# A stack of four graph attention layers on one core: two graphs share every transfer and the order of work is planned anew

## The chip, the cores and the metric

The kernel runs on one core of a Trainium2 chip. The metric is the device time of one execution in microseconds, taken as the median over several runs. One further execution is recorded by the hardware profiler; its span and the durations of its instructions are what the text below reads. The engines are PE (matrix products, results in PSUM), PEld (loading of PE's stationary operand), DVE and ACT (elementwise work and row sums), POOL (elementwise work[...]) and SP, which here only issues transfers.

## The reference, cut to what matters

There are 128 graphs with 128 nodes and 512 features, each with its own 0/1 adjacency matrix. Four attention layers follow each other; each layer adds its result to its input and normalises the rows.

```
x = layernorm(x + gat0(x, adj))       # one head, no weights: attn @ x
x = layernorm(x + gat1(x, adj))       # (a) 4 heads: x @ W1 [512 x 1024], attn, + b1, elu
                                      # (b) 1 head: h @ W2 [1024 x 512], attn, + b2
x = layernorm(x + gat2(x, adj))       # 8 heads of 64: x @ W [512 x 512], attn
x = layernorm(x + gat3(x, adj))       # 1 head: attn @ x, elu
attn = softmax(where(adj, leaky_relu(s_src[i] + s_dst[j], 0.2), -inf))
```

The scores s_src and s_dst are products of the (projected) node features with vectors. Per graph there are 1 + 4 + 1 + 8 + 1 = 15 attention matrices of 128 x 128. All is float32.

## The kernel before

A graph is one tile of 128 rows. `graph(g)` (from L567) lists the operations of graph g: `first` (layer 0), the projection by `w1s`, `second` (four heads), `halves` (the product with W2), `third` (one head of layer 1, then layer 2 with eight heads and layer 3). Each entry is an `Op` with an engine, a duration that the planner uses, buffers read and written, and a function that emits the instructions.

**Attention.** `spread` (L589 to L598) turns columns of destination scores into rows: a DVE transpose, a transfer to DRAM (`row`), and a transfer that broadcasts the rows to all partitions (`db`). `attend` forms the matrix: ACT adds the source score and applies the leaky relu (L646), with the result z in SBUF; DVE subtracts z from the mask and takes the row minimum (L654, one instruction and one read of the accumulator per head); ACT takes the exponential with a row sum (L663). `turned` transposes 128 x 128 blocks: DVE transposes 32 x 32 squares (L607), one transfer writes them to DRAM (L612), and one reads them back in transposed block order (L617 or L622). PE then multiplies by the features (`mixed`, L725; `block`, L896; `heads`, L938).

**Projections.** `project` (L710) chains four matmuls of 128 rows per column group and evicts by ACT (L717). In `second` the four-head projection is 16 matmuls of 258 columns per graph: 512 columns for two heads plus four score columns, in two halves. The product with W2 covers two graphs together: `halves` computes a 2 x 2 block product by Strassen's scheme with seven products of four matmuls of 257 columns (L794) instead of eight. The sums of its left operands are POOL's (L780), the sums of W2's blocks are formed once in the setup. DVE adds partial results (L812), ACT copies others out of PSUM (L807). `norm` is DVE's statistics (L681, L682), ACT's inverse root (L685, L686), a small POOL instruction (L692, for layer 2 also L696) and ACT's scaling (L699). The scores of layer 3 are put together on DVE (L956 to L969).

**What sets the order.** `Pipeline.plan` places the operations of one graph in a period of 28 us, by urgency and with a random shift from a fixed seed. `Pipeline.run` repeats this for all graphs, each 28 us later, and `Pipeline.order` walks through all operations as a list scheduler: an engine takes the earliest operation that can start, not more than AHEAD = 20 us past the oldest one not yet issued. The engines then run their lists strictly in that order and wait on semaphores. Buffers of 128, 512 and 1024 elements a partition share three families of slots (`w128`, `w512`, `w1024`), others have their own; the eight PSUM banks are handed out one at a time. All transfers of the loop are issued by SP: 30 per graph.

**Setup.** Weights are loaded and completed with score columns in the same list, with written times of -20 to 205 us: W1 at once, W2's sums at 109, the eight-head weights `wha` between 70 and 205.

The functions that the change touches, with their lines:

Of the kernel before, what the change touches and what calls it, by code (L numbers as in the profile page):

```python
# [26 lines left out]

PERIOD = 28.0
LATENCY = {"PE": (0.0, 0.8), "DVE": (0.15, 1.44), "ACT": (0.1, 1.44), "POOL": (0.1, 1.44), "SP": (7.06, 7.06)}
FLOW = {"PE": (0.0, 0.6), "DVE": (0.15, 0.8), "ACT": (0.1, 0.8), "POOL": (0.1, 0.8), "SP": (4.5, 4.5)}
AHEAD = 20.0
URGENCY = 0.6
BANKS = 8

SEED, SPREAD = 989, 8.0


class Buf:


    def __init__(self, tag, shape, dtype=F32):
        self.tag, self.shape, self.dtype = tag, shape, dtype
        self.size = 1
        for d in shape[1:]:
            self.size *= d

        if dtype is F32 and shape[0] == P and self.size in (P, 4 * P, 8 * P) and not tag.startswith(("ps", "scr")):  # L50
            self.tag = f"w{self.size}"
        self.ap = self.slot = None

    def view(self, tl):
        if self.tag[0] == "w" and len(self.shape) > 2:
            dims = "abc"[: len(self.shape) - 1]
            tl = tl.rearrange(f"p ({' '.join(dims)}) -> p {' '.join(dims)}", **dict(zip(dims, self.shape[1:])))
        return tl


class Op:
    def __init__(self, engine, cost, emit, ins, outs, extra, uses=(), dma=0.0):
        self.dma = dma
        self.engine, self.cost, self.emit, self.extra = engine, cost, emit, extra
        self.wait = 0
        self.ins, self.outs = ins, outs
        self.uses = list(uses)
        self.bufs = list(dict.fromkeys([*ins, *outs, *uses]))

    def done(self, reader=None):  # L70
        own, other = LATENCY[self.engine]
        return self.cost + self.extra + (own if reader is self.engine else other)


class Pipeline:
    def __init__(self, make, n, place):
        self.make, self.n, self.place = make, n, place

    def plan(self, ops):


        before, after = [set() for _ in ops], [[] for _ in ops]
        last, readers = {}, {}
        for k, op in enumerate(ops):
            for b in op.ins:
                before[k].add(last[b])
            for b in op.outs:
                if b in last:
                    before[k].add(last[b])
                before[k].update(readers.get(b, ()))  # L90
            before[k].discard(k)
            for q in before[k]:
                after[q].append(k)
            for b in op.ins:
                readers.setdefault(b, set()).add(k)
            for b in op.outs:
                last[b], readers[b] = k, set()
        left = [0.0] * len(ops)
        for k in reversed(range(len(ops))):
            left[k] = ops[k].cost + max(  # L100
                (left[q] + ops[k].done(ops[q].engine) - ops[k].cost for q in after[k]), default=0.0
            )
        taken = {e: [] for e in LATENCY}
        times, ready, missing = [0.0] * len(ops), [0.0] * len(ops), [len(q) for q in before]
        waiting = [k for k in range(len(ops)) if not missing[k]]
        rng = random.Random(SEED)
        shift = [SPREAD * rng.random() for _ in ops]
        while waiting:
            k = min(waiting, key=lambda k: (ready[k] - URGENCY * left[k] + shift[k], k))
            waiting.remove(k)  # L110
            op, t = ops[k], ready[k]
            spans = taken[op.engine]
            while True:
                u = t % PERIOD
                clash = [
                    y + d - u for x, y in spans for d in (-PERIOD, 0.0, PERIOD)
                    if u < y + d - 1e-9 and x + d < u + op.cost - 1e-9
                ]
                if not clash:
                    break  # L120
                t += min(clash) + 1e-9
                assert t < ready[k] + 2 * PERIOD, "the period is too short"
            spans.append((t % PERIOD, t % PERIOD + op.cost))
            times[k] = t
            for q in after[k]:
                ready[q] = max(ready[q], t + op.done(ops[q].engine) + max(ops[q].wait, 0) * PERIOD)
                missing[q] -= 1
                if not missing[q]:
                    waiting.append(q)
        return times  # L130

    def run(self, setup):
        times, events = self.plan(self.make(None)), [(t, -1, k, op) for k, (t, op) in enumerate(setup)]
        for g in range(self.n):
            for k, op in enumerate(self.make(g)):
                if op is not None:
                    events.append((g * PERIOD + times[k], g, k, op))
        events.sort(key=lambda e: e[:3])
        for g, op in self.order(events):
            for b in op.outs:  # L140
                if b.ap is None and b.slot is not None:
                    b.ap = self.place(b, g)
            op.emit()

    def order(self, events):

        ops, n = [e[3] for e in events], len(events)
        ends, first, last, readers, open_uses = {}, {}, {}, {}, {}
        before, after = [0] * n, [[] for _ in ops]
        makes, coming = [[] for _ in ops], {}  # L150
        for i, op in enumerate(ops):
            need = {last[b] for b in op.ins + op.uses if b in last}
            for b in op.outs:
                need.update([last[b]] if b in last else [], readers.get(b, ()))
                if b not in first:
                    first[b] = events[i][0]
                    if b.tag != "const":
                        makes[i].append(b)
                        coming.setdefault(b.tag, []).append(i)
            need.discard(i)  # L160
            before[i] = len(need)
            for q in need:
                after[q].append(i)
            for b in op.ins + op.uses:
                readers.setdefault(b, []).append(i)
            for b in op.outs:
                last[b], readers[b] = i, []
            for b in op.bufs:
                open_uses[b] = open_uses.get(b, 0) + 1
                ends[b] = max(ends.get(b, 0.0), events[i][0] + op.done())  # L170

        free = {}
        for b, t in first.items():
            if b.tag != "const":
                places = free.setdefault(b.tag, [])
                s = next((s for s, e in enumerate(places) if e <= t), len(places))
                places[s : s + 1] = [ends[b]]
        assert len(free["ps"]) <= BANKS, "too few banks"
        free = {tag: [(0.0, s) for s in range(BANKS if tag == "ps" else len(p))] for tag, p in free.items()}
        ready, released, clock, lane = [0.0] * n, {}, {e: 0.0 for e in FLOW}, 0.0  # L180
        known = {e: [i for i in range(n) if not before[i] and ops[i].engine == e] for e in FLOW}
        issued, low, out = [False] * n, 0, []

        def start(i):
            t = max(clock[ops[i].engine], ready[i])
            for b in makes[i]:

                rank = 0
                for q in coming[b.tag]:
                    if q >= i or rank >= len(free[b.tag]):  # L190
                        break
                    rank += 1
                if rank >= len(free[b.tag]):
                    return None
                t = max(t, free[b.tag][rank][0])
            return t

        while len(out) < n:
            best = None
            for e, waiting in known.items():  # L200
                found = None
                for i in waiting:
                    if events[i][0] > events[low][0] + AHEAD and i != low:
                        break
                    t = start(i)
                    if t is not None and (found is None or t < found[0]):
                        found = (t, i)
                        if t <= clock[e]:
                            break
# [34 lines left out]
def tile_gat_stack(  # L244
# [63 lines left out]
    def mark():  # L308

        return Buf("const", [P, 1])  # L310
# [740 lines left out]
```

## Time and profile before

| | |
|---|---|
| median of 3 runs | 3246.22 us (3245.11 to 3246.83) |
| span of the profiled execution | 3258.4 us |
| PE busy | 3066.8 us (94%) in 14822 matmuls |
| DVE busy | 2779.0 us (85%) |
| ACT busy | 2451.2 us (75%) |
| POOL busy | 1895.1 us (58%) |
| transfers | 606.08 MB, 75.0% of the time of the 16 DMA engines |
| mean granted clock of PE | 0.976 |

A group of the profile is named by the line of kernel.py, the engine and the instruction, then output<-inputs by tile names, the shape, the count, the busy time, the mean length of one in ns, and the idle time of the engine before it with what ended it. Lengths of neighbours can overlap, so count x mean may exceed the busy time. Tiles of the three shared families all appear as `w`, PSUM banks as `ps`.

### The profile page before, as it was taken

What the parts mean: (1) busy time and instruction counts of PE and PEld (TensorE: products, weight loads), DVE (VectorE), ACT (ScalarE), POOL (GpSimd) and SP (SyncE); (2) the same over time, 40 slices, a digit from 0 to 9 for tenths busy, and PEclk for the clock granted to TensorE, in tenths of its full rate; (3) what the DMA queues carried; (4) which work ended last, traced back from release to release, by engine and by line L of the source; (5) the groups of instructions that cost most, each with busy time, mean ns of one, the idle gap of its engine ahead of it and who ended that gap; (6) DMA issues with size and microseconds to landing.
All of it is one profiled execution on the core that took longest, in us unless ns stands there. A gap on an engine that the chain in (4) does not pass through costs nothing. (4 is left out here: it accounts for less than half of the span.)

```text
span 3258.4 us, 62058 instructions
## 1 busy us (share of the span) xinstructions
PE 3066.8 (94%) x14822; PEld 2488.7 (76%) x14822; DVE 2779.0 (85%) x9833; ACT 2451.2 (75%) x8741; POOL 1895.1 (58%) x2347
## 2 busy tenths in 40 slices
PE   6899999999999999999999999999999999999984
PEld 4688887787777877877777778777787777878853
DVE  4779888888888988898888889889898898989875
ACT  2457787787777777787777877777877777778875
POOL 4655655665565655665555665565566556565533
PEclk7899999999999999999999999999999999999985
DMA  4358777877877877877778777877787787777875
GB/s 119 94 136 196 183 205 188 200 193 190 203 187 188 205 186 192 201 190 200 188 187 200 191 188 204 189 190 201 191 204 187 188 205 188 196 196 190 197 174 129
DMA packets 1657567, 606.08 MB, mean 186 GB/s; under 512 B 1311562, under 2 KB 1508170, under 8 KB 1657204
## 3 DMA queue, kind: packets, MB, share of 16 engines
q1 hardware_dynamic: 1655836, 598.97, 75.0%
q8 instruction: 120, 1.97, 0.2%
q14 instruction: 243, 1.99, 0.2%
q0 software_dynamic: 576, 2.10, 0.2%
q10 hardware_dynamic: 792, 1.06, 0.1%
HBM read 374.43 MB, written 227.48 MB: 185 GB/s over the span
## 5 line engine op out<-in xcount | busy, mean ns | idle before, releaser
L710 PE MATMUL ps<-w1s,w 128*128 128x258 f32 x4096 | 926.9, 384 | 48.5 <-DMA w<-scr 25.0
L710 PEld LDWEIGHTS ps<-w1s,w 128*128 128x128 f32 x4096 | 777.0, 191 | 186.3 <-DVE xl L812 39.5
L654 DVE CUSTOM_DVE_ANT_0 w<-w,w 128x128 f32<-128x128 f32 x1920 | 861.1, 544 | 65.6 <-ACT w L646 49.2
L794 PE MATMUL ps<-w2s,w 128*128 128x257 f32 x3584 | 849.0, 383 | 8.5 <-POOL w L780 8.4
L663 ACT ACTIVATE w<-w,nm 128x128 f32<-128x128 f32 x1920 | 748.0, 394 | 98.2 <-DVE nm L654 76.3
L794 PEld LDWEIGHTS ps<-w2s,w 128*128 128x128 f32 x3584 | 669.1, 191 | 188.8 <-issue 80.0
L646 ACT ACTIVATE w<-w,xl 128x128 f32<-128x128 f32 x1536 | 488.8, 389 | 279.9 <-DMA w<-row 259.1
L607 DVE STREAM_TRANSPOSE w<-w 128x512 f32<-128x512 f32 (+1 forms) x1024 | 551.5, 540 | 34.3 <-ACT w L663 13.3
L710 PE MATMUL ps<-wha,w 128*128 128x273 f32 x2048 | 502.3, 398 | 7.3 <-DMA w<-scr 6.9
L710 PEld LDWEIGHTS ps<-wha,w 128*128 128x128 f32 x2048 | 383.2, 192 | 87.4 <-DVE w L607 6.3
L699 ACT ACTIVATE w<-w,mr,rd 128x512 f32<-128x512 f32 x512 | 415.2, 811 | 33.9 <-POOL mr L692 33.0
L692 POOL TENSOR_SCALAR mr<-mv,rd 128x1 f32<-128x1 f32 x512 | 160.1, 313 | 409.4 <-ACT rd L686 201.8
L663 ACT ACTIVATION_READ_ACCUMULATOR w<-w,nm 128x1 f32 x1920 | 368.1, 192 | 0.0
L681 DVE BATCH_NORM_STATS2 st<-w 128x6 f32<-128x512 f32 x512 | 337.2, 668 | 5.4 <-POOL w L986 4.6
L881 POOL TENSOR_TENSOR xl<-xl,b1t 128x512 f32<-128x512 f32 x256 | 335.2, 1310 | 1.6
L938 PEld LDWEIGHTS ps<-xl,w 128*128 128x128 f32 x2048 | 274.3, 196 | 80.8 <-issue 24.4
L646 ACT ACTIVATE w<-w,sc 128x128 f32<-128x128 f32 x384 | 152.3, 397 | 227.6 <-DMA w<-row 226.6
L725 PE MATMUL ps<-w,w 128*128 128x512 f32 x512 | 277.4, 624 | 32.6 <-DMA w<-scr 31.6
L738 POOL TENSOR_SCALAR w<-adj 128x128 f32<-128x128 int32 x256 | 192.4, 752 | 188.2 <-DMA adj<-in_adj_dram 75.1
L717 ACT COPY xl<-ps 128x258 f32<-128x258 f32 (+1 forms) x768 | 273.2, 362 | 31.8 <-PE ps L710 31.3
L938 PE MATMUL ps<-xl,w 128*128 128x66 f32 x2048 | 265.2, 273 | 27.7 <-DMA w<-scr 14.4
L654 DVE DVE_READ_ACCUMULATOR2_ANT nm<- 128x1 f32 x1920 | 290.5, 151 | 0.0
(213 smaller groups left out, 4258.8 us busy)
## 6 DMA issues: line engine op xcount, KB each, us to landing
scr<-w SPq DMA_DIRECT2D x640, 256.0 KB
w<-scr SPq DMA_DIRECT2D x640, 256.0 KB
w<-row SPq DMA_DIRECT2D x128, 512.0 KB
w<-in_x_dram SPq DMA_DIRECT2D x128, 256.0 KB
w<-row SPq DMA_DIRECT2D x128, 256.0 KB
out_dram<-w SPq DMA_DIRECT2D x128, 256.0 KB
w<-row SPq DMA_DIRECT2D x384, 64.0 KB
scr<-w SPq DMA_DIRECT2D x384, 64.0 KB
```

Of the source, the lines that this page charges most:

```text
L607: op("DVE", 0.12 + 0.133 * n, lambda: nc.vector.transpose(zb.ap.rearrange("p b h c -> p h b c"), src.ap.rearrange("p (h b c) -> p h b c", ...
L646: nc.scalar.activation(z.ap[:, h, :], db.ap[:, h0 + h, :], AF.Prelu, bias=src(h0 + h), alpha=SLOPE)
L654: nc.vector.tensor_tensor_reduce(out=zz.ap[:, h, :].rearrange("p (b a) -> p a b", b=4), in0=z.ap[:, h, :].rearrange("p (a b) -> p a b", b= ...
L663: nc.scalar.activation(zz.ap[:, h, :], zz.ap[:, h, :], AF.Exp, bias=nm.ap[:, h : h + 1], scale=-1.0, accum_out=rs.ap[:, h : h + 1],)
L681: op("DVE", 0.6, lambda: nc.vector.bn_stats(st.ap, y.ap), [y], [st])
L699: op("ACT", 0.7, lambda: nc.scalar.activation(y.ap, y.ap, AF.Identity, bias=mr.ap, scale=rd.ap), [y, rd, mr], [y])
L710: op("PE", w * 4 / 2400 + 0.006, lambda k=k: nc.tensor.matmul(px.ap[:, :w], lhsT=lhs.ap[:, k, :], rhs=wa(k, c), start=(k == 0), stop=(k == ...
L717: op("ACT", 0.06 + w / 1200, lambda: nc.scalar.copy(dst(), px.ap[:, :w]), [px], [t])
L725: op("PE", width * 4 / 2400, lambda: nc.tensor.matmul(pa.ap[:, :width] if len(xv.shape) == 2 else pa.ap.rearrange("p (s c) -> p s c", s=2) ...
L794: return lambda: nc.tensor.matmul(q[b].ap[:, :C2], lhsT=x()[:, k, :], rhs=w2s[:, slot, k, :], start=(fresh and k == 0), stop=(k == 3), ski ...
L881: op("POOL", 1.3, lambda nh=nh: nc.gpsimd.tensor_add(xl.ap[:, nh, : 2 * FH], xl.ap[:, nh, : 2 * FH], b1t[:, nh * 2 * FH : (nh + 1) * 2 * F ...
L938: op("PE", 0.225, lambda u=u, h=h: nc.tensor.matmul(pa.ap[:, u * CH : (u + 1) * CH], lhsT=pt.ap[:, u, :], rhs=xl3.ap[:, h * CH : (h + 1) * ...
```

## The change

The list scheduler, the plan and most of the operations' list are written anew. What differs in the work:

- The unit is a pair of graphs. Every transfer carries both: x, adj, the result, each block transposition (`turned` takes several sources) and each spreading of scores. Layer 2's two groups of four heads of one graph share one transposition. Masks are made for two graphs in one POOL instruction, and the mask of layer 2 is made a second time in `fourth` from a fresh load of adj. The offsets and the score sums of layer 3 for both graphs are small POOL instructions; the latter were DVE's.
- `strassen` replaces both `halves` and the four-head `project`: the pair's two graphs are the rows of the 2 x 2 block product. For the four-head projection it runs twice (two column halves of 258), with two matmuls per product; `w1s` gets seven slots, and `combined` forms the block sums in the setup. The eight-head projection stays a plain product per graph.
- z, the leaky relu's result, is a PSUM bank instead of an SBUF buffer.
- A matmul chain is one operation of the planner instead of one per matmul.
- `plan` gives each operation a due time: the latest start along the longest path to the pair's end, stretched by 1.36, plus 45 us per pair. `lay_out` schedules by due times, with AHEAD = 30, and reckons with POOL and DVE keeping each other waiting (`port`), with descriptor times of transfers and with at most eight transfers under way. At most two Strassen products are open at once.
- Buffers of 64 elements a partition or more lie in one SBUF tile, the arena, at offsets found from the planned times; space is reused 2 us after its planned release.
- The setup's written times end at about 115 us instead of 205.

```diff
+STRETCH, PACE, AHEAD = 1.36, 45.0, 30.0
+HOP = {"PE": 0.0, "DVE": 0.0, "ACT": 1.0, "POOL": 1.0, "SP": 3.0}
+BANKS, PRODUCTS = 8, 2
+LANES = 8
+SLACK = 2.0
...
+def plan(ops):
...
+    for k in reversed(range(len(ops))):
+        left[k] = ops[k].least() + HOP[ops[k].engine] + max((left[q] for q in after[k]), default=0.0)
+    rng = random.Random(SEED)
+    return [STRETCH * (max(left) - left[k]) + SPREAD * rng.random() for k in range(len(ops))]
+
+def lay_out(ops):
...
+            free, best, limit = clock[e], None, ops[line_up[low]].due + AHEAD
+            if e == "SP" and len(landed) >= LANES:
+                free = max(free, landed[-LANES])
+            for due, i in line:
+                t = max(free, ready[i])
+                if due > limit:
+                    break
...
+                if best is None or t < best[0] - REACH:
+                    best = (t, i)
...
+    for b in sorted((b for b in used if b.arena), key=lambda b: (-b.size, b.began)):
...
+            if q.began < b.until + SLACK and b.began < q.until + SLACK:
+                if q.slot - b.slot >= b.size:
+                    break
+                b.slot = max(b.slot, q.slot + q.size)
...
-    w1s = const.tile([P, 4, 2, N1], F32, name="w1s")
+    w1s = const.tile([P, 7, 2, N1], F32, name="w1s")
...
+    w1_ready = combined(18, w1s, w1_ready, ["DVE", "DVE", "DVE", "DVE"])
...
+    def attend(db, h0, nh, src, mask, scaled=False):
+
+        z = bank()
...
+        op("ACT", [0.4] * nh, prelu, [db, src[0]], [z])
+        op("DVE", [0.24] * nh, masked, [z, mask[0]], [zz, nm])
+        op("ACT", [0.387] * nh, exp, [zz, nm], [zz, rs])
...
+    def strassen(left, s, w, nk, wide, cols, to, out, ready):
+
+        pa, pb, pc = bank(), bank(), bank()
...
+        product(pa, left[0][0], 0, True)
...
+        taken(pa, t1)
+        product(pc, left[0][1], 1, True)
+        added(pc, t1, 0, 0)
+        product(pa, s[1], 4, False)
+        product(pb, s[0], 3, True)
+        taken(pa, u2)
+        taken(pb, v)
+        product(pa, s[2], 5, False)
+        product(pb, s[3], 2, False)
+        added(pa, v, 1, 1)
+        added(pb, u2, 0, 1)
+        product(pa, left[1][1], 6, False)
+        copied(pa, wide, lambda: to(1, 0), joins=[out[1]])
...
+        def normed():
+            nc.gpsimd.tensor_add(sc4.ap, sc4.ap, sz.ap)
+            nc.gpsimd.tensor_mul(sc4.ap, sc4.ap, rd.ap.unsqueeze(2).to_broadcast([P, 2, 2]))
+            nc.gpsimd.tensor_mul(sw.ap, swf.ap.unsqueeze(1).to_broadcast([P, 2, 2]), md.ap.unsqueeze(2).to_broadcast([P, 2, 2]))
+            nc.gpsimd.tensor_add(sc4.ap, sc4.ap, sw.ap)
...
+    def pair(n):
+        st = first(n)
+        xT = st["xT"]
+        xl = [Buf("xl1", [P, 2, N1]) for _ in G]
+        left = [[part(xT, slice(4 * g + 2 * a, 4 * g + 2 * a + 2)) for a in range(2)] for g in G]
+        s = sums(left, [P, 2, P])
+        for j in range(2):
+            cols = slice(j * C1, (j + 1) * C1)
+            strassen(left, s, w1s, 2, C1, cols, lambda g, h, cols=cols: xl[g].ap[:, h, cols], xl, w1_ready)
+        hT = second(st, xl)
+        xl2 = Buf("xl2", [P, 2, 2, C2])
+        left = [[part(t) for t in both] for both in hT]
+        strassen(left, sums(left, [P, 4, P]), w2s, 4, C2, slice(0, C2), lambda g, h: xl2.ap[:, g, h, :], [xl2, xl2], w2_ready)
+        third(st, xl2)
...
```

## The prediction

> **What bounds the kernel now.** I read the engine totals first, then windows of the span, the rows of the steady stretch, the waits, and one stretch of the timeline. Windows over the ramp, the steady part and the drain (busy us and instruction count for PE, PEld, DVE, ACT, POOL, then clock and DMA share):
>
> ```profile
> 0.00:150.00 150.00, 111.17 (x382) 76.49 (x382) 89.18 (x259) 51.55 (x157) 92.04 (x98) 0.82 0.40 108
> 150.00:300.00 150.00, 147.80 (x728) 124.08 (x726) 120.40 (x387) 97.38 (x338) 80.44 (x89) 1.00 0.64 155
> 300.00:3000.00 2700.00, 2609.49 (x12856) 2135.26 (x12855) 2376.62 (x8493) 2115.03 (x7597) 1613.76 (x2008) 1.00 0.79 194
> 3000.00:3258.00 258.00, 198.32 (x862) 152.84 (x860) 192.79 (x697) 187.22 (x653) 108.82 (x154) 0.82 0.69 167
> ```
>
> In the middle 2700 us PE is busy 96.6% at full clock; DVE follows with 88%, DMA 79%, ACT 78%, POOL 60%. One graph issues 115 matmul instructions (each f32 matmul is two: 32 first projection, 28 second, 16 third, 6 mixing, 16 and 16 for the heads, 1 turn), so 12856/115 = 111.8 graphs passed: 24.15 us a graph, 48.3 a pair of graphs, 46.7 of it PE busy and 1.6 idle. The ramp and the drain cost the rest: 3258.4 - 64 x 48.3 = 167 us.
>
> Rows of PE and of the two dearest groups of DVE and ACT in the steady stretch (busy us, mean ns, idle before and its releasers):
>
> ```profile
> L710 PE MATMUL ps<-w1s,w 128*128 128x258 f32 x3583 | 805.8, 383 | 47.7 <-DMA w<-scr 25.0 <-DVE ri L671 9.3 <-DVE st L681 8.4
> L794 PE MATMUL ps<-w2s,w 128*128 128x257 f32 x3136 | 740.2, 382 | 1.4 <-POOL w L780 1.4
> L654 DVE CUSTOM_DVE_ANT_0 w<-w,w 128x128 f32<-128x128 f32 x1677 | 742.6, 539 | 47.2 <-ACT w L646 30.9 <-DMA row<-w 11.2 <-ACT w L663 3.8
> L646 ACT ACTIVATE w<-w,xl 128x128 f32<-128x128 f32 x1338 | 426.0, 389 | 262.5 <-DMA w<-row 241.8 <-issue 7.0 <-DVE mv L682 4.3
> ```
>
> A matmul instruction against w1s occupies PE for 805.8/3583 = 0.225 us; one against w2s, a column narrower, takes 0.236, so about 0.011 x 56 = 0.6 us a pair is waiting that the busy figure hides. PE's visible waits are small and spread: operands still in a transfer, or late from DVE. ACT waits mainly for broadcast rows in flight.
>
> The timeline shows why DVE is long (start, length; first DVE's masked sums, then POOL in the same stretch):
>
> ```profile
> 1601.14 1.26 DVE L654 CUSTOM_DVE_ANT_0 w<-w,w 128x128 f32<-128x128 f32 x1
> ...
> 1602.25 1.19 DVE L654 CUSTOM_DVE_ANT_0 w<-w,w 128x128 f32<-128x128 f32 x1
> ...
> 1603.30 1.42 DVE L654 CUSTOM_DVE_ANT_0 w<-w,w 128x128 f32<-128x128 f32 x1
> ...
> 1604.57 0.37 DVE L654 CUSTOM_DVE_ANT_0 w<-w,w 128x128 f32<-128x128 f32 x1
> ```
> ```profile
> 1600.88 1.27 POOL L862 TENSOR_TENSOR w<-w,b2t 128x512 f32<-128x512 f32 x1
> 1602.11 1.09 POOL L673 TENSOR_TENSOR w<-w,ri 128x512 f32<-128x512 f32 x1
> 1603.16 1.31 POOL L780 TENSOR_TENSOR w<-w,w 128x512 f32<-128x512 f32 x1
> ```
>
> Each long masked sum ends just after the POOL instruction that overlaps it; the one without such an overlap takes 0.37 us. The median of the line is 0.382, the mean 0.539.
>
> **What the Trainium skill says.** "SBUF — State Buffer", section "Who interferes with whom": a VectorE instruction with two SBUF inputs contends with a GpSimd instruction that reads SBUF and the later one blocks for the whole instruction; with at most one SBUF input, outside the two-port modes, it does not. The timeline agrees: 1.19 to 1.42 us against 0.37. "ScalarE: Activation LUTs", section "Step-by-step: what each stage is for": ScalarE writes PSUM with lower latency than SBUF. No ACT instruction of this trace writes PSUM. "PSUM — Partial Sum Buffer", section "PSUM bank collisions raise a hardware error": two engines may not touch one bank in the same partitions at once, whatever the columns. No run here shows that yet; it bears on a bank that ACT fills and DVE drains. "DMA: Bandwidth & Descriptors", section "Anatomy of one DMA — SWDGE (gpsimd) path": about 2 us of a transfer are fixed. It is said of GpSimd-issued transfers; the shortest on the chain of waits here, SP-issued, takes 2.57 us for 64 KB, which is close.
>
> **The change part by part**, per pair of graphs.
>
> *PE.* Strassen on the four-head projection: 2 column halves x 7 products x 2 = 28 f32 matmuls for 32, 8 instructions less: 8 x 0.225 = 1.8 us. Everything else keeps count and width (second 28, third 16 of 273 columns, mixing 6, heads 16 and 16). Two graphs in one transpose changes nothing. PE busy: 46.7 - 1.8 = 44.9. Sum of this part: 64 x 1.8 = 115 us.
>
> *DVE*, now 2376.6/2700 x 48.3 = 42.5. With its first input in PSUM a masked sum has one SBUF input: 30 x (0.539 - 0.382) = -4.8. The four tail score instructions go to POOL or merge: L959, L969 and L966 at 0.636, 0.270, 0.252, twice: -2.3. Fewer reciprocals (9 for 12 at 0.142), one mask product and one score shift for two: -0.8. Nine Strassen additions instead of four, at the 0.403 of L812: +2.0. Sum 36.6. Whether a PSUM input slows the sum is not shown; L903 with one takes 0.663 for 512 columns, L681 without takes 0.667, so I take nothing; bounds -1 and +2.
>
> *ACT*, now 37.8: 16 evictions for 15, +0.36. Prelu into PSUM is unknown: from -0.1 us each (the skill's hint, sized by guess from the 0.389 of L646) to +0.075 (four of them take 1.26 us in the timeline, 0.315 apiece, because they overlap; without overlap each is 0.389). So -3 to +2.2; I take +1.5. Sum 39.7.
>
> *POOL*, now 28.9: four operand sums of 256 columns at half of L780's 1.28, +2.6; masks of 256 columns, four for six of 0.75 to 0.83, +0.5; six small score instructions at about the 0.26 of L696, +1.6; norm offsets, eight small ones for ten, -0.9. Sum 32.7.
>
> *Transfers.* A graph now issues 30 on SP (the page's issue counts of the loop sum to 3840); a pair will issue 4 + 11 + 16 = 31 for 60. At medians of 0.42 to 0.64 us each that frees some 15 us of SP a pair, and 29 fixed latencies. Bytes stay, so DMA share rises with the pace only: 0.79 x 48.3/45.7 = 0.83. A transfer of eight heads lasts longer than one of four, but the order has about ten pairs in flight (the plan spreads a pair's steps over some 450 us of due time and starts one every 45), which covers it; without that cover each of the six doubled round trips costs 2 to 3 us on a pair's chain, which is paid only in the drain.
>
> *Order and arena.* They have no instructions. They decide how much of PE's waiting stays: 1.6 visible + 0.6 hidden a pair. DVE gets slack (88% to 80%), SP gets slack, ACT loses some (78% to 87%). I take half the 2.2 as recovered, less 0.3 for new waits (coarser hand-offs, arena space reused 2 us after its planned release): -0.8. Bounds: +2 and -2.2.
>
> *Ramp and drain.* Weights are due earlier (the last at 115 instead of 205), and the seven w1s slots need four more subtractions first, about 4 x 1.2 = 5 us, hidden behind the first graph's attention. Pairs enter two graphs at a time, and after the last third projection a longer eight-head chain runs alone, where PE cannot be filled: +15. The ramp should give about that back. I take 0, bounds -40 and +60.
>
> **Sum.** Pace 48.3 - 1.8 - 0.8 = 45.7; 64 x 45.7 = 2925; plus 167 = 3092 us of span, against 3258.4. The median of the runs stands at 3246.2/3258.4 = 0.9963 of the span: 3081, say **3080**.
>
> **Rivals.** (1) *PE stops waiting*: 44.9 less the hidden 0.6 is 44.3 a pair. 64 x 44.3 + 155 = 2990 of span, 2980; up to 3035 for the case. For it: ten pairs in flight, and an order that reckons with the shared port. Against: DVE at 80% and ACT near 87% in fixed order have never run without waits here.
> (2) *The gain goes into the ends and new waits*: the Strassen saving stands, nothing of the waiting is recovered, the ends cost +60: 64 x 46.5 + 227 = 3203, 3190; 3130 to 3235.
> (3) *Slower, by the bank hand-off*: ACT fills a bank with four heads, and DVE may not read the first head until the fourth is written, while the new order books them head by head. In order, DVE stands while it waits: at the 0.315 a head of today's prelu, 0.95 for each of six four-head attentions and 0.3 for each of three two-head ones, 6.6 us a pair, DVE 43.2 of 45.7, still no bound. It decides when DVE's standing passes 48.3 - 36.6 = 11.7 us a pair, that is 1.3 an attention, because ACT's prelus are queued behind other exponentials: 12.5 us give a pace of 49.1 and 3298. Against: DVE has other ready work most of the time.
> (4) *No change*: only by a chance cancellation of these.
>
> **How the numbers follow.** Forecast 0.52 (own range 3035 to 3130), rival 1 0.13, rival 2 0.17, rival 3 0.16, rival 4 0.02. Differences under 0.2% are about what a measurement of this kernel cannot tell from none. Faster 0.82, same 0.02, slower 0.16. The range 3000 to 3220 leaves out part of rival 1, the top of rival 2 and rival 3, about 0.2.
>
> **What would show it.** Right: 3584 matmul instructions in the first projection for 4096; masked sums with a mean near 0.4 us and a PSUM input; 1984 loop transfers on SP for 3840; a steady pace of 45 to 46.5 us a pair with PE at 97% or more; DVE near 80%. Wrong: masked sums waiting on the prelu for more than 10 us a pair; a ramp or drain over 200 us together; ACT over 95%; PE waits on transfers above 100 us in the steady part.

## The result, and the profile after

The changed kernel takes 3542.16 us (median; 3540.49 to 3544.96) against 3246.52 us: a ratio of 1.0903, 95% interval 1.0878 to 1.0928. It is slower by 296 us, and outside the forecast range. (A fourth run of the kernel before moved its median from the 3246.22 us above.)

The windows of the changed kernel over the ramp and the steady part, in the columns shown for before:

```profile
0.00:300.00 300.00, 229.56 (x943) 175.66 (x944) 186.01 (x588) 132.61 (x428) 161.44 (x175) 0.88 0.50 123
300.00:2800.00 2500.00, 2251.77 (x10600) 1811.23 (x10598) 1774.83 (x6670) 1801.48 (x6100) 1435.17 (x1903) 0.95 0.79 179
```

A pair now issues 222 matmul instructions, so 10600/222 = 47.75 pairs pass in 2500 us: 52.4 us a pair against 48.3 before and 45.7 forecast. PE is busy for 47.2 of them, at a granted clock of 0.95, and idle for 5.2. No other engine is full either: DVE 71%, ACT 72%, POOL 57%, DMA 79%.

The steady rows of PE, DVE and ACT (300 to 3200 us) that answer to those of before:

```profile
L710 PE MATMUL ps<-w2s,arena 128*128 128x257 f32 x3110 | 771.8, 402 | 198.7 <-DVE arena L755 178.8 <-DVE nm L653 12.6 <-ACT arena L718 4.8
L710 PE MATMUL ps<-w1s,arena 128*128 128x258 f32 x3080 | 762.7, 400 | 86.5 <-ACT ps L646 40.5 <-ACT arena L718 17.9 <-DVE arena L939 16.0
L653 DVE CUSTOM_DVE_ANT_0 arena<-ps,arena 128x128 f32<-128x128 f32 x1668 | 451.6, 380 | 84.8 <-ACT ps L646 50.9 <-issue 29.8
L646 ACT ACTIVATE ps<-arena 128x128 f32<-128x128 f32 x1328 | 487.4, 370 | 140.0 <-DMA arena<-row 79.3 <-DVE arena L939 20.9 <-DVE nm L653 7.3
```

The masked sum (now L653) fell from a mean of 0.539 to 0.380 us, as worked out, and the leaky relu into PSUM from 0.389 to 0.370. But the instructions against w1s and w2s are longer in the mean (0.400 and 0.402 us for 0.383 and 0.382), and PE waits for DVE's additions.

The lines that the rest of the text names: L597 is DVE's transpose of score columns (sT), L601 the transfer of the score rows to DRAM, L606 their broadcast; L619, L623 and L632 are the block transpose on DVE, its write to DRAM and its read-back; L672 is POOL's scaling by the inverse row sum, L755 the Strassen additions, L879 the elu, L939 the scaling of the eight heads, L718 ACT's evictions, L807 the load of x. Why DVE is late, the waits of POOL, DVE and SP say (what waited, for what, us in total, times, longest):

```profile
POOL arena L672 <- DMA row<-arena: 293.3, 48, 8.1
...
DVE arena L619 <- POOL arena L672: 235.5, 87, 8.7
DVE arena L619 <- DMA row<-arena: 120.4, 19, 7.8
DVE arena L939 <- DMA row<-arena: 99.2, 28, 10.4
...
SPq L601 <- DMA arena<-row: 263.7, 54, 6.9
...
SPq L601 <- DMA arena<-in_x_dram: 88.8, 36, 3.7
```

L601 sends the score rows to DRAM. It reads columns that DVE has just transposed (sT). It has no business with a load of x into another buffer, nor L672, a product of two buffers on chip, with a row transfer. Yet L601 waits for other transfers into the arena, 137 times in 55.4 pairs, and L672, L619 and L939 wait for L601's transfer. The timeline of SP shows one such place, and POOL, DVE and PE behind it (start, length, idle before):

```profile
1524.88 2.97 SPq L807 DMA_DIRECT2D arena<-in_x_dram  x1
1531.72 0.56 SPq L601 DMA_DIRECT2D row<-arena  x1
```
```profile
1533.65 1.61 POOL L672 TENSOR_TENSOR arena<-arena,ri 128x256 f32<-128x256 f32 x2 [6.94 <-DMA row<-arena]
```
```profile
1534.30 0.45 DVE L619 STREAM_TRANSPOSE arena<-arena 128x256 f32<-128x256 f32 x1 [7.43 <-POOL arena L672]
```
```profile
1536.37 3.79 PE L710 MATMUL ps<-w2s,arena 128*128 128x257 f32 x8 [5.80 <-DVE arena L755]
```

SP issues nothing between 1527.85 and 1531.72, where L601 waits 3.7 us for the load of x; then POOL, DVE and PE resume one after the other, after 6.9, 7.4 and 5.8 us.

### The profile page after: what moved, and what is told of

The parts are those of the page before. It is cut to its first block, busy times and chain, and to the rows that moved or that the text cites. A ratio compares the mean times of both kernels' runs of the same rounds, so it can differ in the third digit from the quotient of the medians.

```text
span 3541.5 us, 56054 instructions
## 1 busy us (share of the span) xinstructions
PE 3079.7 (87%) x14310; PEld 2463.1 (70%) x14310; DVE 2438.6 (69%) x9073; ACT 2440.3 (69%) x8229; POOL 1977.9 (56%) x2603
## 3 DMA queue, kind: packets, MB, share of 16 engines
q10 hardware_dynamic: 792, 1.06, 0.1%
## 5 line engine op out<-in xcount | busy, mean ns | idle before, releaser
L710 PE MATMUL ps<-w2s,arena 128*128 128x257 f32 x3584 | 888.4, 402 | 233.6 <-DVE arena L755 198.3
L710 PEld LDWEIGHTS ps<-w2s,arena 128*128 128x128 f32 x3584 | 702.0, 200 | 385.9 <-DVE arena L755 213.6
L710 PE MATMUL ps<-w1s,arena 128*128 128x258 f32 x3584 | 885.6, 400 | 94.3 <-ACT ps L646 42.9
L710 PEld LDWEIGHTS ps<-w1s,arena 128*128 128x128 f32 x3584 | 700.3, 199 | 302.3 <-issue 60.7
L718 ACT COPY arena<-ps 128x258 f32<-128x258 f32 (+2 forms) x1024 | 356.6, 374 | 726.6 <-PE ps L710 272.5
L619 DVE STREAM_TRANSPOSE arena<-arena 128x512 f32<-128x512 f32 (+1 forms) x832 | 504.5, 629 | 444.3 <-POOL arena L672 266.5
L662 ACT ACTIVATE arena<-arena,nm 128x128 f32<-128x128 f32 x1920 | 742.7, 394 | 6.3 <-DVE nm L653 6.2
L646 ACT ACTIVATE ps<-arena 128x128 f32<-128x128 f32 x1536 | 563.0, 370 | 165.0 <-DMA arena<-row 97.7
L653 DVE CUSTOM_DVE_ANT_0 arena<-ps,arena 128x128 f32<-128x128 f32 x1920 | 520.1, 380 | 130.6 <-ACT ps L646 87.0
L733 POOL TENSOR_TENSOR arena<-arena 128x256 f32<-128x256 f32 (+1 forms) x512 | 490.4, 975 | 151.9 <-issue 98.2
L710 PE MATMUL ps<-wha,arena 128*128 128x273 f32 x2048 | 499.8, 395 | 25.3 <-DMA arena<-scr 25.3
L672 POOL TENSOR_TENSOR arena<-arena,ri 128x512 f32<-128x512 f32 (+1 forms) x192 | 172.5, 913 | 394.6 <-DMA row<-arena 312.5
L653 DVE DVE_READ_ACCUMULATOR2_ANT nm<- 128x1 f32 x1920 | 289.1, 151 | 0.0
```

The lines of the kernel that those rows point to most:

```text
L619: op("DVE", 0.075 + 0.134 * m, lambda a=a, src=src: nc.vector.transpose(zb.ap[:, :, a * m : (a + 1) * m, :].rearrange("p b h c -> p h b c" ...
L646: nc.scalar.activation(z.ap[:, h * P : (h + 1) * P], db.ap[:, h0 + h, :], AF.Prelu, bias=src[1]()[:, h : h + 1], alpha=SLOPE)
L653: nc.vector.tensor_tensor_reduce(out=zz.ap[:, h, :].rearrange("p (b a) -> p a b", b=4), in0=z.ap[:, h * P : (h + 1) * P].rearrange("p (a b ...
L662: nc.scalar.activation(zz.ap[:, h, :], zz.ap[:, h, :], AF.Exp, bias=nm.ap[:, h : h + 1], scale=-1.0, accum_out=rs.ap[:, h : h + 1],)
L710: nc.tensor.matmul(px.ap[:, :w], lhsT=lhs(k), rhs=rhs(k), start=(fresh and k == 0), stop=(k == nk - 1), skip_group_check=True,)
L718: op("ACT", 0.04 + w / 1200, lambda: nc.scalar.copy(to(), px.ap[:, :w]), [px], outs, joins)
```

## The experiments

Theory A: the arena is one tile, and a read of sT out of it (every 32nd partition) is ordered by the program's semaphores against accesses to other parts of the tile, so that one score transfer waits for whatever is under way into the arena and later writers wait for it. Theory B: SP, in its fixed order, waits behind the larger transfers. Theory C: the hand-off of PSUM banks from ACT to DVE costs the time.

The experiments fall into three series on three chips, on which the kernel before took 3223, 3259 and 3252 us; with the result above it took 3247. So each ratio is to the kernel before of the same series, and times from different series can be compared to about 1% only.

**e1_scores_own**

```diff
-SLACK = 2.0
+SLACK = 1.5
...
-        self.arena = shape[0] == P and self.size >= 64 and tag not in ("ps", "const") and not tag.startswith("scr")
+        self.arena = shape[0] == P and self.size >= 64 and tag not in ("ps", "const") and not tag.startswith(("scr", "sT"))
```

> The changed kernel with the transposed score columns (sT) in tiles of their own instead of the arena; to make room, arena space is reused 1.5 us after its planned release instead of 2.0. Order and instructions are the same. Theory A (the read of sT out of the arena is taken to touch all of it, so that one score transfer per pair waits for all transfers under way into the arena and later writes wait for it): SP's waits of L601 on other loads and the waits of POOL and DVE on that transfer go, PE idles 1.5 to 2.5 us a pair instead of 5.2, the pace falls from 52.3 to 46.5 to 48 us, time 3160 to 3270. Theory B (SP's fixed order with transfers twice as large makes everything stand behind read-backs): the waits move to L632 and L606, time 3450 to 3540. Theory C (the PSUM bank hand-off of the leaky relu): no change, 3540.

Measured: 3096.15 us, ratio 0.9615 (0.9591 to 0.9638). It is faster than both kernels, and faster than theory A's own range. Its windows:

```profile
300.00:2800.00 2500.00, 2475.25 (x12320) 2037.21 (x12319) 2086.69 (x7769) 2094.47 (x7088) 1694.34 (x2221) 1.00 0.91 208
2800.00:3093.00 293.00, 204.69 (x952) 162.53 (x951) 172.72 (x654) 194.24 (x647) 133.23 (x195) 0.82 0.71 151
```

12320/222 = 55.5 pairs, 45.05 us a pair, PE busy 99% at full clock. SP's waits in its steady part (300 to 2800 us):

```profile
SPq L632 <- DMA scr<-arena: 206.4, 88, 4.7
SPq L601 <- DVE arena L755: 173.0, 47, 7.4
SPq L606 <- DMA row<-sT: 137.1, 70, 3.8
```

SP still waits for read-backs, as long as before (L632 had 246.6 us in 2900), and it costs nothing now: theory B falls. L601 no longer waits for other transfers. Theory C had required no change and falls too.

**e1b_scores16_own and e1c_slack**

```diff
-        self.arena = shape[0] == P and self.size >= 64 and tag not in ("ps", "const") and not tag.startswith("scr")
+        self.arena = shape[0] == P and self.size >= 64 and tag not in ("ps", "const") and not tag.startswith(("scr", "sT16"))
```

with SLACK at 1.9 (e1b); only SLACK at 1.5 (e1c).

> As e1_scores_own, but only the 16-row sT of the eight-head layer leaves the arena (space reused after 1.9 us). Theory A, if only that one transfer is at fault: within 1% of e1_scores_own. If the smaller ones matter too: between it and 3540. Theories B and C: 3450 to 3540.

> The changed kernel with space of the arena reused 1.5 us after its planned release instead of 2.0, nothing else. Theory A: the reuse distance is not the cause, 3540 within 1%. Rival D (reuse of arena space before its late readers are done is the cause): slower, 3580 or more.

Measured: e1b 3246.9 us, 1.0073 (1.0049 to 1.0097). In its trace L601 still waits 286 us of 2500 for broadcast rows on their way into the arena, so the smaller score transfers seem to matter too; the run also has another SLACK than e1_scores_own, and its time alone doesn't show it. e1c 3249.18 us, 1.0085 (1.0055 to 1.0116). This missed both expectations: reusing space earlier did no harm, but it took 293 us off. It moves buffers to other offsets and makes the arena narrower (32192 elements a partition for 32744), so it could not tell which of the two did it. With the same SLACK and on the same chip e1_scores_own is 153 us faster than e1c: that much goes with sT's own tiles, though these move the other buffers again. The next runs change the width alone.

**e5_arena_24_wider, e6_arena_1_wider, e9_arena_16_wider**

```diff
-        arena = work.tile([P, max(b.slot + b.size for o in order for b in o.bufs if b.arena)], F32, name="arena")
+        arena = work.tile([P, 24 + max(b.slot + b.size for o in order for b in o.bufs if b.arena)], F32, name="arena")
```

with 24, 1 and 16. Offsets, instructions and order stay; only the waits that the program gets differ.

> The changed kernel with the arena 24 elements wider (32768 for 32744 a partition), nothing else: every buffer lies at the same offset, every instruction and the order are the same. Counted in the compiled programs, the transfer of the 16 score rows waits on 0.05 other transfers on average instead of 4.95, the two-row ones on 0.40 instead of 1.25. Theory A in its sharper form (the width decides which strided reads out of the arena are taken to meet other parts of it): pace 45 to 46 us a pair, PE over 97% busy in the steady part, time within 1.5% of e1_scores_own, 3080 to 3150. Theory A' (what lies in the arena is reused too early, and moving sT out only shifted the places): no change, 3540.

> The changed kernel with the arena one element wider (32745), nothing else. In the compiled program the 16-row transfer waits on 4.98 others, the two-row ones on 3.36 instead of 1.25. Theory A: slower than the changed kernel, 3600 to 4000, since three more score transfers per pair wait for what is under way. Theory A': 3540.

> The changed kernel with the arena 16 elements wider (32760). In the compiled program the waits are as in the changed kernel (4.95, 1.25 and 1.06 other transfers for those of 16, 2 and 8 rows). If the waits decide and not the width as such: 3540 within 1%. If any widening helps: 3140.

Measured:

| arena, elements a partition | other transfers that a score transfer of 16, 2, 8 rows waits on (mean, in the compiled program) | us | ratio and interval |
|---|---|---|---|
| 32744 (the change) | 4.95, 1.25, 1.06 | 3542.16 | 1.0903 (1.0878 to 1.0928) |
| 32745 (e6) | 4.98, 3.36, 0.58 | 4319.2 | 1.325 (1.3223 to 1.3277) |
| 32760 (e9) | 4.95, 1.25, 1.06 | 3547.4 | 1.0901 (1.0861 to 1.0941) |
| 32768 (e5) | 0.05, 0.40, 0.98 | 3137.66 | 0.9627 (0.9611 to 0.9643) |

The unneeded waits decide. Twenty-four unused elements take 404 us off (415 by the ratios), one adds 777, and sixteen, which leave the waits as they were, change nothing. The traces show the difference as well. These are the separate wait instructions of L601 and its transfers in 2500 us, first of the changed kernel, then of e6 and of e5:

```profile
L601 SPq EVENT_SEMAPHORE  x325: 17/28/3674, 299.2 to 2797.0; - x163
L601 SPq DMA_DIRECT2D row<-arena x239: 521/556/2200, 300.6 to 2797.1; - x120
```
```profile
L601 SPq EVENT_SEMAPHORE  x486: 17/28/10828, 306.2 to 2794.4; - x162
L601 SPq DMA_DIRECT2D row<-arena x192: 503/554/573, 308.2 to 2794.4; - x192
```
```profile
L601 SPq DMA_DIRECT2D row<-arena x275: 533/555/2122, 306.1 to 2798.3; - x138
L601 SPq EVENT_SEMAPHORE  x113: 17/17/860, 308.6 to 2796.9; - x113
```

That is 1.4, 2.5 and 0.4 waits a transfer. Counted as in the table, e1c has 0.95, 0.32 and 0.95 and e1b 0.05, 1.41 and 1.05: e1c had lost most of the 16-row transfer's waits without meaning to, and e1b had kept those of the two-row ones. e6 went beyond its expected 4000. Its ACT waits in the steady part show the row transfers in front of everything:

```profile
ACT arena L718 <- DMA row<-arena: 397.3, 67, 9.9
...
ACT arena L662 <- DMA row<-arena: 107.2, 34, 5.9
ACT arena L701 <- DMA row<-arena: 104.3, 40, 4.2
```

In e5, 12133 instructions in 2500 us give 45.7 us a pair, as expected. POOL's and DVE's waits of L672 and L619 for row transfers are gone. DVE's waits of L939 for one are left, 1.6 us a pair where the changed kernel had 1.8:

```profile
DVE arena L939 <- DMA row<-arena: 88.3, 33, 5.5
```

The trace of e9, as slow as the changed kernel, has none of these. So of the waits shown for the changed kernel it was not L939's that cost the time.

**e3_leaky_in_sbuf and e8_scores_own_slack_1**

```diff
-        z = bank()
+        z = Buf("z", [P, nh * P])
```

on e1_scores_own, with SLACK at 1.0; e8 is e1_scores_own with SLACK at 1.0 and nothing else.

> e1_scores_own with the leaky relu's result z in the arena instead of a PSUM bank (arena space reused after 1.0 us to make room). The forecast's step: 30 masked sums a pair at about 0.54 us instead of 0.38, DVE +4.8 us a pair, from about 37.6 to 42.4 of 45: PE stays the bound with some more waits, +0.5 to +2 us a pair, 3130 to 3230. If the PSUM bank matters more, because DVE then bounds in this order: over 3250. If it does not matter: 3096.

> e1_scores_own with arena space reused 1.0 us after its planned release instead of 1.5, as e3_leaky_in_sbuf had it. If what e3 lost came from the leaky relu's place: 3096 within 0.7%. If it came from early reuse: 3250 or more.

Measured: e3 3364.11 us, 1.0317 (1.0302 to 1.0333); e8 3103.66 us, 0.9536 (0.9513 to 0.956). e3 lies above the 3130 to 3230 that the forecast's step gave, and beyond the 3250 from which on DVE was expected to bound, so the step was priced too low. Early reuse costs nothing; with z in SBUF this kernel is 8.2% slower (1.0317/0.9536). The windows and DVE's dearest group of e3, steady part:

```profile
300.00:2800.00 2500.00, 2299.33 (x11165) 1858.86 (x11166) 2235.29 (x7040) 1855.96 (x6436) 1579.75 (x2016) 0.99 0.84 189
```
```profile
L653 DVE CUSTOM_DVE_ANT_0 arena<-arena 128x128 f32<-128x128 f32 x1508 | 766.8, 619 | 10.2 <-ACT arena L646 5.7 <-ACT arena L718 0.2
```

The masked sums of e1_scores_own and of e3 one by one (count: shortest, median and longest in ns):

```profile
L653 DVE CUSTOM_DVE_ANT_0 arena<-ps,arena x1662: 341/383/408, 312.7 to 2796.5; 128x128 f32<-128x128 f32 x185
```
```profile
L653 DVE CUSTOM_DVE_ANT_0 arena<-arena x1508: 339/385/1504, 302.9 to 2790.0; 128x128 f32<-128x128 f32 x189
```

With both inputs in SBUF a masked sum has a mean of 0.619 us. The median is that of e1_scores_own; the mean grows through single ones of up to 1.504 us, where with z in PSUM none passes 0.408. DVE is busy for 44.4 us a pair instead of 37.6, and the pace falls to 49.7: with DVE at 89% in a fixed order PE waits for it (71.0 us for L879, 49.4 for L755). So without the PSUM step this order is slower than the old kernel. Not all of the 8.2% need be the place itself: e3's plan was made anew, still books a masked sum at 0.24 us and does not reckon there with POOL and DVE keeping each other waiting. A plan that knows of it was not tried.

**e4_plain_four_heads, e7_scores_own_again, e10_plain_four_heads_again**

```diff
-        s = sums(left, [P, 2, P])
-        for j in range(2):
-            cols = slice(j * C1, (j + 1) * C1)
-            strassen(left, s, w1s, 2, C1, cols, lambda g, h, cols=cols: xl[g].ap[:, h, cols], xl, w1_ready)
+        for g in G:
+            project(
+                part(xT, slice(4 * g, 4 * g + 4)),
+                lambda k, c: w1s[:, SLOT[k // 2, c // 2], k % 2, c % 2 * C1 : (c % 2 + 1) * C1], KF, C1, 4,
+                lambda c, g=g: xl[g].ap[:, c // 2, c % 2 * C1 : (c % 2 + 1) * C1], xl[g], w1_ready,
+            )
```

on e1_scores_own, without `combined` for w1s; e7 is e1_scores_own once more, e10 the kernel of e4 beside it.

> e1_scores_own with the four-head projection as four plain products per graph and column group instead of Strassen's seven per pair: 8 matmul instructions more a pair at 0.225 us, no operand sums on POOL, six additions less on DVE. PE at 99% busy in e1_scores_own: +1.8 us a pair, +115 us, 3190 to 3230. If PE were not the bound there: 3096 to 3130.

> The kernel of e1_scores_own once more, beside e8, e9 and e10 on one chip, since the kernel before differed by 1% between the chips of the first two series. If PE bounds it, its time does not depend on the chip: 3090 to 3105, whatever the kernel before takes here.

> The kernel of e4_plain_four_heads beside e7 on one chip. From the paces of the steady parts, 46.35 against 45.05 us a pair: 64 x 1.3 = 83 us over e7, 3165 to 3190. If the chip made that difference: 40 us over e7.

Measured: e4 3178.22 us, 0.9745 (0.973 to 0.9759); e7 3106.93 us, 0.9555 (0.9519 to 0.959); e10 3173.55 us, 0.9758 (0.9731 to 0.9784). e4 missed both of its expectations: Strassen was worth less than 115 us, but more than nothing. e7 lies 2 us above its range: the kernel of e1_scores_own takes the same on two chips within 0.4%, where the kernel before differs by 0.9%. Beside each other, Strassen is worth 3173.55 - 3106.93 = 67 us, not 115. The steady windows of e7 and of e10:

```profile
300.00:2800.00 2500.00, 2468.96 (x12265) 2027.09 (x12264) 2076.75 (x7723) 2081.93 (x7054) 1684.70 (x2209) 1.00 0.91 207
```
```profile
300.00:2800.00 2500.00, 2493.41 (x12408) 2063.84 (x12407) 1934.56 (x7222) 2028.82 (x6901) 1518.02 (x1942) 1.00 0.91 202
```

A plain pair has 230 instructions: 53.95 pairs, 46.34 us each, against 55.25 pairs of 45.25. PE is busy 46.2 against 44.7 a pair, but idle 0.1 against 0.6. So 1.5 of PE's work are saved and 0.4 given back as waiting. That the sums and additions cause this waiting, and not the order, which is planned anew here, was not tested by itself.

## Why the prediction was wrong

**The step that failed is "Order and arena".** It took -0.8 us a pair and bounded the effect at +2. If the rest of the forecast's sum is left as it is, the measured pace makes the term 52.4 - (48.3 - 1.8) = +5.9. Against e5, which differs by 24 unused elements, the changed kernel loses 52.4 - 45.7 = 6.6 us a pair, some 400 us in all. The arena was priced as a matter of when space is reused. It was a matter of which accesses the program orders against each other. None of the rivals named it. What could have been asked ahead: one score transfer reads every 32nd partition of a tile that nearly everything shares, and SP issues its transfers in a fixed order, so whatever makes that one wait holds the others too.

**Rival 3 had the right sign for a wrong reason.** It alone forecast a slower kernel. DVE's waits for the leaky relu in its bank (L653 for L646) come to 50.9 us in 2900, 0.9 a pair, where 11.7 would have decided.

**With the waits gone, the forecast of the pace holds.** e5, which takes nothing but waits from the changed kernel, runs at 45.7 us a pair, as forecast; its 3138 us lie above 3080 mostly because the ends take 3135.7 - 64 x 45.74 = 208 us instead of 167. That the pace fits to the digit is in part luck, since the terms below are off both ways. e1_scores_own runs at 45.05 us a pair, between the forecast 45.7 and rival 1's 44.3, with PE at 99%. Its 3096 us are close to the forecast 3080, but partly by two errors that cancel: the pace is worth 42 us less than forecast, the ends 3092.9 - 64 x 45.05 = 210 us instead of 167. The first 300 us hold 244 us of PE work against 259 before, so the ramp gave nothing back, and the last 293 us only 205.

**Terms, against the steady part of e1_scores_own.** PE busy 44.6 (forecast 44.9). DVE 37.6 (36.6). ACT 37.7 (39.7): the prelu into PSUM costs 0.02 us less apiece instead of 0.05 more. POOL 30.5 (32.7). DMA share 0.91 (0.83): 41.0 us of DMA time a pair against 38.2 before, although the bytes are the same; I had let only the pace count. The 1252864 packets of 128 bytes took 13.0 ns each in the kernel before and 16.4 ns in e1_scores_own; why is open. The masked sum's step was right in mechanism and too small: 0.16 us apiece from the old kernel, 0.24 when taken back in the new one, and 6.8 us of DVE a pair for 4.8. Strassen's 8 instructions were counted rightly (3584), and worth 1.5 us of PE for 1.8. Two slips of the prediction change nothing: 30 x (0.539 - 0.382) is 4.7, not 4.8, and the short masked sum of its timeline did have a POOL instruction beside it, L692 on one column (0.44 us from 1604.46); what it lacked was a long one.

**Of the tests named ahead**, the count of matmuls and the masked sums' mean came true in the changed kernel. Pace, PE share and DVE share came true only without the unneeded waits. Of the four signs of being wrong, none occurred in the changed kernel, though it was wrong: DVE's waits on the prelu were 0.9 us a pair, the ends took 3541.5 - 64 x 52.36 = 190 us, ACT stood at 72%, and PE waited for no transfer itself. It waited for DVE, which waited for POOL, which waited for the transfer: a list of one engine's own waits doesn't show a wait handed on.

**The two statements of the Trainium skill behind these terms.** "SBUF — State Buffer", section "Who interferes with whom", says that a VectorE instruction with two SBUF inputs contends with POOL's reads of SBUF, and one with a single SBUF input does not: e3 agrees, with 0.619 us in the mean for two SBUF inputs against 0.382 for one. "ScalarE: Activation LUTs", section "Step-by-step: what each stage is for", calls PSUM the destination of lower latency: the traces agree, with 0.370 us in the changed kernel against 0.389 before and 0.390 in e3, both of which write SBUF.

**What stays open.** Why a width of 32745 or 32744 makes the strided read meet other buffers and 32768 does not was not traced into the program that derives the waits. In e1c_slack the waits of L601, the places of the buffers and the width changed together, and which share of its 293 us is whose was not separated.

## What to carry to other kernels

When many buffers become slices of one tile, look in the profile at what each engine waits for: a transfer that waits on loads it doesn't use, or an on-chip product that waits on a transfer it has nothing to do with, is an order that the data doesn't need. Keep whatever is read with a step over partitions in a tile of its own. Two cheap runs find it out: the same kernel with the suspect taken out of the shared tile, and with the tile padded by a few unused elements.

## What the runs showed of the hardware that was not expected

PE's granted clock fell with its gaps: 1.00 in the steady part with PE 99% busy, 0.95 at 90% (the changed kernel) and 0.86 at 80% (e6), with the w2s instruction at a mean of 0.381, 0.401 and 0.458 us. The usual instruction did not change. The same instruction in the changed kernel and in e1_scores_own (count: shortest, median and longest in ns):

```profile
L710 PE MATMUL ps<-w2s,arena x2688: 377/380/797, 308.5 to 2791.5; 128*128 128x257 f32 x192
```
```profile
L710 PE MATMUL ps<-w2s,arena x3099: 377/379/484, 299.8 to 2780.0; 128*128 128x257 f32 x194
```

The long ones stand behind a long gap, as here, in the place shown above:

```profile
1523.33 7.25 PE L710 MATMUL ps<-w2s,arena 128*128 128x257 f32 x32
1536.37 3.79 PE L710 MATMUL ps<-w2s,arena 128*128 128x257 f32 x8 [5.80 <-DVE arena L755]
1539.96 3.11 PE L779 MATMUL ps<-arena 128*128 128x512 f32 x4
1542.90 3.64 PE L710 MATMUL ps<-w1s,arena 128*128 128x258 f32 x16
```

Ahead of the gap an instruction occupies PE for 0.23 us, behind it for 0.47, and 6.5 us later for 0.23 again. PE is busy for 47.2 us a pair in the changed kernel and for 44.6 in e1_scores_own, with the same 222 instructions: the 5.2 idle us a pair go with some 2.5 more in slower matmuls. The length of the single gap seems to count more than the sum: e3 is idle for 8% of its steady part, in gaps of at most 2.8 us, and kept a clock of 0.99, where the changed kernel, idle for 10% with gaps of up to 7.1 us, had 0.95. At which length the clock falls was not measured.

And DMA ran at a share of 0.91 without becoming the bound (e1_scores_own, PE at 99%), while in the changed kernel it stayed at 0.79 and moved 179 GB/s for 208.
